# Two graph layers on one core: the second layer's first gathers read a copy of its table that lacks three node tiles

## The chip, the core and the metric

The kernel runs on one core of a Trainium2 chip. The metric is device microseconds of one execution, the median of the timed runs. The engines are named as in the profile: PE (TensorE, the matrix products), DVE (VectorE), ACT (ScalarE), POOL (GpSimd) and SP (SyncE, which here only issues transfers). Every engine works through its own queue in order and waits at semaphores for the others.

## What is computed

The inputs are 6250 nodes with 128 features and 200,000 edges, sorted by their destination. Two layers follow each other, both over the same edges:

```python
h = relu(layernorm(x))
z = (h @ W).reshape(N, 8, 16)                 # layer 0: graph attention, 8 heads
e = leaky_relu(el[src] + er[dst], 0.2)
a = exp(e - segment_max(e, dst)[dst])
agg = segment_sum(z[src] * a, dst) / segment_sum(a, dst)
x = x + agg + bias
h = relu(layernorm(x))
s, v = h @ W_up (scalar and vector part)      # layer 1: messages by tensor product
w0..w3 = silu(silu(edge_feats @ A1 + b1) @ A2 + b2) @ A3
m = products of s[src], v[src], edge_attrs and w0..w3   # 256 numbers an edge
x = x + segment_sum(m, dst) / 10 @ W_out
```

What matters here is `z[src]` and `s[src], v[src]`: for every edge a row of a table is fetched by the number of its source node. The sources are in no order, so layer 1 can read any row of its table from its first edge on.

## The kernel before

**Tables and gathers.** `t0` (136 floats a node) and `t1` (128 floats a node) are tables in DRAM. `t0` is complete before layer 0 starts. `t1` is written by layer 0, node tile by node tile. The edges form 1563 tiles of 128; 16 tiles are a block, and there are 98 blocks. `gather` (L830) issues one indirect DMA on POOL for each edge tile: 128 rows of the table into one tile's place of a buffer. Buffers come from `z_pool`, five of them, each for one block; block 0 of layer 0 has a buffer of its own, `z_first`. `gathered` takes the next buffer of the pool and fills it. In 31 blocks (`by_row`, every third) the last tile isn't gathered; SP fetches its 128 rows one by one (`rows_by_row`, L1067), three blocks ahead.

**Layer 0.** The loop over `g` (L1346) handles one group of tiles, nearly always a block, in each pass: `logits` of group g, the maxima over each destination, `weights`, `weighted` and `sums` of group g - 1, and every second pass the node work for the node tile that group g - 2 completed: `node_x`, `node_d`, `node_h`, `node_t` and `node_s`, which ends with `sv`, a node tile's 128 rows of `t1`. `node_out` (L1281) stores `sv` into `t1`, from SP, at the top of the next pass. There are 50 node tiles. After the loop the last four groups are written out by hand (L1410 to L1464). Tile 46 is stored first there, tile 47 after the sums of group 95 have been carried on, and tiles 48 and 49 together at the very end. Block 97 is cut into a group of 3 tiles and one of 8.

**Layer 1.** It works in units of four edge tiles (391 of them). For each unit: `network`, one step of the edge network for the next block (`p_h` in PSUM); `tensor_weights`, the last product of that network; `messages` (DVE, L1532 to L1541), which reads the gathered rows; `one_hot`; and `sums1` (PE, L1549), which adds the unit's messages to its block's sums. `edge_rows` loads the edge inputs of a block from SP. `take_rows(b + 2)` stands at the first unit of block b. `node1` and `node_out1` close a node tile.

**Order.** The queues of PE, DVE, ACT and SP keep the order of the program within a layer (`manual_schedule`). POOL's gathers keep theirs too, and run ahead as far as buffers are free. Tiles of DRAM are tracked like others: a gather from `t1` waits for every store to `t1`.

**Pools.** What both layers or layer 0 alone need stands in the pool `fconst`, which stays open to the end. `s_pool` and `row_pool` are opened after a pool named `fbuild`, in which the masks are built, has been closed; they lie where it lay.

Of the kernel before, what the change touches and what calls it, by code (L numbers as in the profile page):

```python
# [18 lines left out]
P = 128  # L19
H = 8  # L20
D = 16
F = H * D
# [3 lines left out]
MW = 8 * MU  # L26
# [3 lines left out]
KB = 16  # L30
# [705 lines left out]
W0 = 32  # L736
PRE = 1.0 / math.sqrt(MU)
# [4 lines left out]
def tile_even_edges(  # L742
# [28 lines left out]
    nc = tc.nc  # L771
    NX = xp.shape[0] // P
    TU = n_tiles
    TG = -(-TU // P)
# [5 lines left out]
    keep = ctx.enter_context(tc.tile_pool(name="keep", bufs=1))  # L780
    t0 = dram.tile([NX * P - W0, ZW], F32, name="ft0")
    t1 = dram.tile([NX * P - W0, P], F32, name="ft1")

    def rows(i):

# [41 lines left out]
        nc.vector.scalar_tensor_tensor(mr[:m], mv[:m, :, 0:1], -1.0, rs[:m], op0=OP.mult, op1=OP.mult)  # L827
        return rs, mr

    def gather(to, table, tiles, width):  # L830
        for k, t in enumerate(tiles):
            nc.gpsimd.indirect_dma_start(  # L832
                out=to[:, k, :width], out_offset=None, in_=table,
                in_offset=bass.IndirectOffsetOnAxis(ap=src_col[:, t : t + 1], axis=0))
        return to
# [128 lines left out]
def even_edges(tc, v):  # L964
    nc = tc.nc
    NX, TU, TG, NB, KT, MC = (v[k] for k in (
        "NX", "TU", "TG", "NB", "KT", "MC"))
    t0, t1, ident, eps, er3, z_first, dstt, nums = (v[k] for k in (
        "t0", "t1", "ident", "eps", "er3", "z_first", "dstt", "nums"))
    xp, dstc, y4, f8, bias, out, moments, deviation, normal, gather, tiles_of = (v[k] for k in (  # L970
        "xp", "dstc", "y4", "f8", "bias", "out", "moments", "deviation", "normal", "gather", "tiles_of"))
    with ExitStack() as ctx:
        const = ctx.enter_context(tc.tile_pool(name="fconst", bufs=1))
        z_pool = ctx.enter_context(tc.tile_pool(name="fz", bufs=5))

        def gathered(table, tiles, width):
            return gather(z_pool.tile([P, KB, ZW], F32, name="g"), table, tiles, width)

        iota = const.tile([P, P], F32, name="fiota")
        nc.sync.dma_start(iota, nums[:, NB * KB + TG : NB * KB + TG + P])  # L980
        jp = const.tile([P, P], F32, name="fjp2")
        nc.sync.dma_start(jp, nums[:, NB * KB + TG + P :])
        rsel = const.tile([P, P // KB, P], BF, name="frsel")
        nc.sync.dma_start(rsel, v["rsel"])
        x_all = const.tile([P, NX, P], F32, name="fx_all")
        bias_b = const.tile([P, F], F32, name="fbias_b")
# [16 lines left out]
        identb = const.tile([P, P], BF, name="fidentb")  # L1003
        nc.vector.tensor_copy(identb, ident)

        er3o = const.tile([P, NX, 3, H], BF, name="fer3o")
        nc.sync.dma_start(er3o[:WB, :, :, :], er3[WB:, :, :, :])
        nc.sync.dma_start(er3o[WB:, : NX - 1, :, :], er3[:WB, 1:, :, :])
        shift = const.tile([P, 3, P], F32, name="fshift")
        for k, by in enumerate((-H, P - H, H)):  # L1010
            nc.vector.tensor_single_scalar(shift[:, k, :], jp, float(by), op=OP.is_equal)
        masks = const.tile([P, TG, MC], BF, name="fmasks")
# [25 lines left out]
        s_pool = ctx.enter_context(tc.tile_pool(name="fs", bufs=16))  # L1038

        by_row = [b for b in range(3, NB - 2) if b % 3 == 0]
        row_pool = ctx.enter_context(tc.tile_pool(name="frow", bufs=3))
        at = [const.tile([P, P], I32, name=f"fat{i}") for i in range(2)]
        with tc.tile_pool(name="fat_ps", bufs=1, space=PSUM) as at_ps:
            col = const.tile([P, P], F32, name="fcol")
# [44 lines left out]
        def finish(b, p_u, width, carry, agg, pool):  # L1091

            if b % 2 == 0:
                agg = pool.tile([P, MW], F32, name="agg")
            o = agg[b % 2 * WB : b % 2 * WB + WB, :width]
            if carry is None:
                nc.vector.tensor_copy(o, p_u[:WB, :width])
            else:
                nc.vector.tensor_add(o, p_u[:WB, :width], carry[:, :width])
            carry = pool.tile([WB, MW], F32, name="carry")  # L1100
            nc.scalar.copy(carry[:, :width], p_u[WB:, :width])
            return carry, agg


        in_order = {mybir.EngineType.PE, mybir.EngineType.DVE, mybir.EngineType.Activation,
                    mybir.EngineType.SP}
        with tc.manual_schedule(engines=in_order), \
# [160 lines left out]
            def node_s(u):  # L1268
                i, n, p_n = u["i"], u["n"], u["p_n"]
                for j in range(n):  # L1270
                    nc.tensor.matmul(p_n[:, 2 + j, :], u["h_t"][:, j, :], wup, start=True, stop=True)
                sv = u["sv"] = l0n.tile([P, 2, P], F32, name="sv")
                nc.scalar.activation(sv[:, :n], p_n[:, 2 : 2 + n], AF.Copy, scale=PRE)

            def node_out(u):
                i, n, sv = u["i"], u["n"], u["sv"]
                first = i * P - W0
                if i == 0:
                    nc.sync.dma_start(t1[: P - W0, :], sv[W0:, 0, :])
                else:  # L1280
                    nc.sync.dma_start(t1[first : first + n * P].rearrange("(j p) f -> p j f", p=P),  # L1281
                                      sv[:, :n])

            groups = [(b, 0, KB) for b in range(NB - 1)]
            cut = min(3, KT[-1] - 1)
# [1 line left out]
            shift_to = {}  # L1287
            for _, _, kt in groups:
                if kt * H not in shift_to:
                    sh = const.tile([P, P], F32, name=f"fshift{kt}")  # L1290
# [45 lines left out]
            er_sum(cs[0])  # L1336
            for q in range(4):
                ends_of(cs[1], q)
            st = {"ends": const.tile([P, 2, MW], F32, name="fends")}
# [71 lines left out]
            for n in late:  # L1411
                node_out(n)
            with_bias(NX - 2, 2)

            logits(c3)
            masks_of(c2)
# [45 lines left out]
            node_out(u)  # L1462
            for step in (node_d, node_h, node_t, node_s, node_out):
                step(w)  # L1464


        with tc.manual_schedule(engines=in_order), \
# [106 lines left out]
            both = l1n.tile([P, 2, MW], F32, name="both", bufs=1)  # L1574
            nc.vector.memset(both[WB:, 1, :], 0.0)

            blk = [{} for _ in range(NB)]
            us = [{"b": b, "k0": k0, "m": min(4, KT[b] - k0)}
                  for b in range(NB) for k0 in range(0, KT[b], 4)]
            NU = len(us)  # L1580

            def take_rows(b):
                if b < NB:
                    blk[b]["z"] = gathered(t1, range(b * KB, b * KB + KT[b] - (b in by_row)), P)

            rows, rows_until.n, late = rows_by_row(1, t1, P), 0, []
            for b in range(2):
                edge_rows(b)
                take_rows(b)
            for step in range(4):  # L1590
                network(0, step)
            tensor_weights(us[0])
# [4 lines left out]
            for i, u in enumerate(us):  # L1597
                b, k0, m = u["b"], u["k0"], u["m"]
                if k0 == 0:
                    take_rows(b + 2)  # L1600
                    filled(1, b, blk[b]["z"], P)
                    edge_rows(b + 2)
                if k0 == 4:
                    while late:
                        node_out1(late.pop())
                rows_until(rows, b + (k0 + 4) / KB)
                if b + 1 < NB:
                    network(b + 1, k0 // 4)
# [177 lines left out]
```

## Time and profile before

| | |
|---|---|
| timed runs, median of 3 | 3916.27 us (3915.74 to 3917.14) |
| profiled execution | 6201.12 us, span 6199.2 us |
| mean granted PE clock, profiled | 0.692 |
| PE busy, share of the span | 2970.3 us, 48% |
| POOL busy | 2919.2 us, 47% |
| DVE busy | 2207.9 us, 36% |
| ACT busy | 1390.7 us, 22% |

The profiled execution is 1.58 times as long as a timed run. Its durations of single instructions can be used; its waits have to be read with care, because a timed run has 2285 us less of them. In the timeline each line gives the start in us from the beginning of the span, the length, the engine, the line of the kernel, the operation and its tiles; the brackets give the idle time before it and what ended that. In the trace both tables are called `ft` (`ft0`, `ft1`), the table of source numbers `fsrc`, and gathered buffers `g` or `fz_first`. [...]

### The profile page before, as it was taken

The numbers are of one execution on the slowest core, as the hardware profiler recorded it, in microseconds if no ns is written. First come the engines' busy times: TensorE is split into PE (matmuls) and PEld (weight loads), VectorE is DVE, ScalarE is ACT, GpSimd is POOL, SyncE is SP. The second block draws the span as 40 slices with busy tenths as digits, with TensorE's granted clock in tenths as the row PEclk, the third lists the DMA queues.
The fourth block names the chain that finished last, engine by engine and source line by source line (L and its number), as shares of the span: only waits on it lengthen the run. The fifth ranks groups of instructions, "written<-read, shape, count | busy, mean of one in ns | idle before, by whom it ended". The sixth has DMA issues, their size and how long they took to land. (4 is left out here: it accounts for less than half of the span.)

```text
span 6199.2 us, 62249 instructions
## 1 busy us (share of the span) xinstructions
PE 2970.3 (48%) x14593; PEld 2462.3 (40%) x14593; DVE 2207.9 (36%) x5379; ACT 1390.7 (22%) x3612; POOL 2919.2 (47%) x3096
## 2 busy tenths in 40 slices
PE   2444434334443434444445555555555555555557
PEld 1333333333333333433334444444444444444445
DVE  3332323223232322232234334443344434443346
ACT  2212112112121212122112222222222222222223
POOL 6354454544445444454534444444444444444442
PEclk6666666656666665665677777777777777777778
DMA  5111111111111111111111111111111111111110
GB/s 133 31 41 39 39 41 40 40 41 39 39 40 42 40 39 40 39 41 39 39 30 35 38 38 37 37 37 37 38 37 36 35 39 38 36 36 37 39 38 25
DMA packets 188124, 249.35 MB, mean 40 GB/s; under 512 B 77888, under 2 KB 137952, under 8 KB 187744
## 3 DMA queue, kind: packets, MB, share of 16 engines
q0 software_dynamic: 98048, 207.27, 14.1%
q1 hardware_dynamic: 89408, 37.92, 2.4%
q8 instruction: 118, 1.93, 0.1%
q14 instruction: 262, 2.15, 0.1%
q10 hardware_dynamic: 288, 0.07, 0.0%
HBM read 234.73 MB, written 9.99 MB: 39 GB/s over the span
## 5 line engine op out<-in xcount | busy, mean ns | idle before, releaser
L832 POOL DMA_INDIRECT g<-ft,fsrc x3048 | 2885.4, 947 | 3174.9 <-issue 1510.7
L1549 PE MATMUL p_u<-mj,s 128*128 128x256 f32 x3126 | 925.2, 448 | 719.5 <-DVE mj L1541 601.3
L1549 PEld LDWEIGHTS p_u<-mj,s 128*128 128x128 f32 x3126 | 679.9, 225 | 905.1 <-DVE mj L1541 656.2
L1221 PE MATMUL p_u<-g,s 128*128 128x136 f32 x3062 | 621.5, 382 | 42.5 <-issue 39.6
L1221 PEld LDWEIGHTS p_u<-g,s 128*128 128x128 f32 x3062 | 588.6, 285 | 48.9 <-issue 44.9
L1534 DVE TENSOR_TENSOR p_w<-g,p_w 128x128 f32<-128x128 f32 x391 | 114.7, 293 | 1278.6 <-ACT p_w L1516 1099.6
L1516 ACT ACTIVATE p_w<-p_w,yb 128x64 f32<-128x64 f32 x1563 | 451.1, 289 | 475.1 <-remote 250.9
L1149 PEld LDWEIGHTS <-d 128*128 128x128 bf16 x1563 | 99.2, 113 | 845.1 <-ACT d L1140 512.0
L1512 PE MATMUL p_w<-fa3p,h 128*128 128x256 f32 x1564 | 427.4, 398 | 0.0
L1140 ACT CAST d<-p_d 128x512 bf16<-128x512 f32 x391 | 228.1, 587 | 881.3 <-remote 746.2
L1502 ACT ACTIVATE h<-p_h,fb 128x512 f32<-128x512 f32 x196 | 134.9, 688 | 1167.9 <-remote 841.8
L1512 PEld LDWEIGHTS p_w<-fa3p,h 128*128 128x128 f32 x1564 | 306.3, 206 | 142.3 <-issue 103.1
L1560 PE MATMUL p_n<-fwout,m_t 128*128 128x128 f32 x192 | 57.1, 451 | 561.6 <-ACT m_t L1558 561.6
L1138 PE MATMUL p_d<-fident,s 128*128 128x128 f32 x1563 | 320.1, 357 | 5.2 <-issue 5.2
L1216 DVE TENSOR_TENSOR g<-g,pe 128x1024 f32<-128x1024 f32 x193 | 226.2, 1213 | 226.2 <-ACT g L1207 155.4
L1499 PE MATMUL p_h<-h,fa2p 128*128 128x512 f32 x392 | 245.9, 714 | 125.2 <-ACT h L1497 98.7
L1532 DVE TENSOR_TENSOR vy<-g,p_i 128x384 f32<-128x384 f32 x391 | 215.0, 550 | 218.0 <-ACT p_i L1491 216.3
L1497 ACT ACTIVATE h<-p_h,fb 128x512 f32<-128x512 f32 x196 | 134.6, 687 | 698.2 <-PE p_h L1495 391.4
L1155 DVE TENSOR_REDUCE p_n<-p_er 128x128 f32<-128x384 f32 (+1 forms) x97 | 54.7, 563 | 663.6 <-remote 257.3
L1149 PE MATMUL p_er<-fer,d 128*128 128x24 bf16 x784 | 55.3, 185 | 467.7 <-ACT d L1140 285.2
L1086 DVE TENSOR_TENSOR s<-p_i,fdloc 128x512 f32<-128x512 f32 x391 | 269.0, 688 | 14.0 <-ACT h L1497 14.0
L1138 PEld LDWEIGHTS p_d<-fident,s 128*128 128x128 f32 x1563 | 258.2, 192 | 39.3 <-issue 30.6
(185 smaller groups left out, 3478.5 us busy)
## 6 DMA issues: line engine op xcount, KB each, us to landing
r<-ft SPq DMA_DIRECT2D x3968, 0.5 KB
r<-ft SPq DMA_DIRECT2D x3968, 0.5 KB
g<-ft,fsrc POOLq DMA_INDIRECT x3048
ft<-in_e_f_dram SPq DMA_DIRECT2D x98, 64.0 KB
yb<-in_e_y_dram SPq DMA_DIRECT2D x98, 32.0 KB
fx_all<-in_e_xp_dram SPq DMA_DIRECT2D x48, 64.0 KB
ft<-sv SPq DMA_DIRECT2D x47, 64.0 KB
out_dram<-fx_all SPq DMA_DIRECT2D x47, 64.0 KB
```

Of the source, the lines that this page charges most:

```text
L832: nc.gpsimd.indirect_dma_start(out=to[:, k, :width], out_offset=None, in_=table, in_offset=bass.IndirectOffsetOnAxis(ap=src_col[:, t : t + ...
L1086: nc.vector.tensor_tensor(s[:, :m], iota[:, None, :].to_broadcast([P, m, P]), dloc[:, t : t + m].unsqueeze(2).to_broadcast([P, m, P]), OP. ...
L1138: nc.tensor.transpose(p_d[:, k, :], c["s"][q][:, k, :], ident)
L1140: nc.scalar.copy(d[:, :m], p_d[:, :m])
L1149: nc.tensor.matmul(c["p_er"][:, 4 * q + k].rearrange("p s h -> p (s h)"), c["d", q][:, k, :], er_w, start=True, stop=True)
L1216: nc.vector.tensor_mul(zh, zh, p_a[:, k0 : k0 + m].unsqueeze(3).to_broadcast([P, m, H, D]))
L1221: nc.tensor.matmul(c["p_u"][:, :ZW], c["s"][k // 4][:, k % 4, :], c["z"][:, k, :], start=c["o"] + k == 0, stop=c["o"] + k == KT[c["b"]] - 1)
L1499: nc.tensor.matmul(p_h.rearrange("p q e -> p (q e)"), a2p, c["h1"].rearrange("p q e -> p (q e)"), start=True, stop=True)
L1512: nc.tensor.matmul(w[:, k : k + n].rearrange("p k a u -> p (k a u)"), c["h2"][q // 4][:, q % 4, :], a3p[:, :n].rearrange("p k f -> p (k f) ...
L1516: nc.scalar.activation(w[:, k, ::2, :], w[:, k, ::2, :], AF.Copy, scale=c["yb"][:, k0 + k, 0:1])
L1532: nc.vector.tensor_mul(vy, v_n, y_p)
L1549: nc.tensor.matmul(blk[b]["p_u"][:, :MW], u["s"][:, k, :], u["mj"][:, k, :], start=k0 + k == 0, stop=k0 + k == KT[b] - 1)
```

## The change

A second table, `t1z`, is written beside `t1`. Node tiles 0 to 46 are stored into both. Tiles 47, 48 and 49 of `t1z` are zero: zeros are stored there once, in the setup. The rows of these three tiles stay in SBUF (`sv_late`).

The first 24 edge tiles of layer 1 are gathered from `t1z` in place of `t1`: block 0 into `z_first`, and half of block 1 into a buffer of the pool. These gathers stand in the program after tile 46's stores. An edge whose source lies in the last three node tiles gets a row of zeros this way, and the missing row is added on the chip: for four edge tiles at a time, PE spreads the source numbers over the partitions (4 products), DVE compares them with the numbers of the three tiles' nodes (3 comparisons), PE multiplies the resulting zeros and ones by `sv_late` (12 products), and DVE adds the result to the gathered rows. This runs one to two units ahead of the unit that reads the rows, six times in all. The other tiles of block 1 and all later ones come from `t1`.

The pools are ordered anew: `s_pool` and `row_pool` are opened before `fbuild`, and what layer 0 alone needs (`rsel`, `masks`, `er3o` and others) moves from `fconst` to a pool `l0c`, closed before layer 1.

The diff, cut to what the prediction speaks of:

```diff
+    t1z = dram.tile([NX * P - W0, P], F32, name="ft1z")
...
-    def gather(to, table, tiles, width):
-        for k, t in enumerate(tiles):
+    def gather(to, table, tiles, width, first=0):
+        for k, t in enumerate(tiles, first):
...
         z_pool = ctx.enter_context(tc.tile_pool(name="fz", bufs=5))
+        s_pool = ctx.enter_context(tc.tile_pool(name="fs", bufs=16))
+        row_pool = ctx.enter_context(tc.tile_pool(name="frow", bufs=3))
+        of_l0 = ctx.enter_context(ExitStack())
+        l0c = of_l0.enter_context(tc.tile_pool(name="l0c", bufs=1))
...
+        NL, NE = 3, 24
+        LATE = NX - NL
...
-        rsel = const.tile([P, P // KB, P], BF, name="frsel")
+        rsel = l0c.tile([P, P // KB, P], BF, name="frsel")
...
+            zeros = build.tile([P, NL, P], F32, name="fzeros")
+            nc.vector.memset(zeros, 0.0)
+            nc.sync.dma_start(t1z[LATE * P - W0 :].rearrange("(j p) f -> p j f", p=P), zeros)
...
+        sv_late = const.tile([P, NL, P], F32, name="fsv_late")
...
-                sv = u["sv"] = l0n.tile([P, 2, P], F32, name="sv")
-                nc.scalar.activation(sv[:, :n], p_n[:, 2 : 2 + n], AF.Copy, scale=PRE)
+                if i < LATE:
+                    sv = u["sv"] = l0n.tile([P, 2, P], F32, name="sv")[:, :n]
+                else:
+                    sv = u["sv"] = sv_late[:, i - LATE : i - LATE + n]
+                nc.scalar.activation(sv, p_n[:, 2 : 2 + n], AF.Copy, scale=PRE)
...
-                if i == 0:
-                    nc.sync.dma_start(t1[: P - W0, :], sv[W0:, 0, :])
-                else:
-                    nc.sync.dma_start(t1[first : first + n * P].rearrange("(j p) f -> p j f", p=P),
-                                      sv[:, :n])
+                for table in (t1, t1z) if i < LATE else (t1,):
+                    if i == 0:
+                        nc.sync.dma_start(table[: P - W0, :], sv[W0:, 0, :])
+                    else:
+                        nc.sync.dma_start(
+                            table[first : first + n * P].rearrange("(j p) f -> p j f", p=P), sv)
...
             with_bias(NX - 2, 2)
+            early = {0: gather(z_first, t1z, range(KB), P),
+                     1: gathered(t1z, range(KB, NE), P)}
...
+        of_l0.close()
...
+            place = l1n.tile([P, NL], F32, name="place", bufs=1)
+            for j in range(NL):
+                nc.vector.tensor_scalar(place[:, j : j + 1], jp[:, 0:1], -1.0,
+                                        float((LATE + j) * P - W0), op0=OP.mult, op1=OP.add)
+            src_f = l1n.tile([P, NE], F32, name="src_f", bufs=1)
+            nc.vector.tensor_copy(src_f, v["src_col"][:, :NE])
+
+            def late_ends(t):
+
+                if t < NE:
+                    p_h = l1_ps.tile([P, 4, P], F32, name="p_h")
+                    for k in range(4):
+                        nc.tensor.matmul(p_h[:, k, :], src_f[:, t + k : t + k + 1].to_broadcast([P, P]),
+                                         ident, start=True, stop=True)
+                    oh = late_ends.of[t] = l1n.tile([P, NL, 4, P], F32, name="oh")
+                    for j in range(NL):
+                        nc.vector.tensor_scalar(oh[:, j], p_h, place[:, j : j + 1], None,
+                                                op0=OP.is_equal)
+
+            late_ends.of = {}
+
+            def late_rows(t):
+                if t < NE:
+                    z, k0, oh = blk[t // KB]["z"], t % KB, late_ends.of.pop(t)
+                    p_n = l1_ps.tile([P, 4, P], F32, name="p_n", bufs=1)
+                    for k in range(4):
+                        for j in range(NL):
+                            nc.tensor.matmul(p_n[:, k, :], oh[:, j, k, :], sv_late[:, j, :],
+                                             start=j == 0, stop=j == NL - 1)
+                    z = z[:, k0 : k0 + 4, :P]
+                    nc.vector.tensor_add(z, z, p_n)
...
             def take_rows(b):
-                if b < NB:
+                if b in early:
+                    blk[b]["z"] = gather(early[b], t1, range(max(b * KB, NE), b * KB + KB), P,
+                                         max(NE - b * KB, 0))
+                elif b < NB:
                     blk[b]["z"] = gathered(t1, range(b * KB, b * KB + KT[b] - (b in by_row)), P)
...
                 take_rows(b)
+            for t in (0, 4):
+                late_ends(t)
+            late_rows(0)
             for step in range(4):
                 network(0, step)
...
                     tensor_weights(us[i + 1])
+                late_ends(4 * (i + 2))
                 messages(u)
+                late_rows(4 * (i + 1))
```

More of the change, by code (lines that the diff above doesn't have):

```diff
@@ L967, in even_edges @@
         "NX", "TU", "TG", "NB", "KT", "MC"))
-    t0, t1, ident, eps, er3, z_first, dstt, nums = (v[k] for k in (
-        "t0", "t1", "ident", "eps", "er3", "z_first", "dstt", "nums"))
+    t0, t1, t1z, ident, eps, er3, z_first, dstt, nums = (v[k] for k in (
+        "t0", "t1", "t1z", "ident", "eps", "er3", "z_first", "dstt", "nums"))
     xp, dstc, y4, f8, bias, out, moments, deviation, normal, gather, tiles_of = (v[k] for k in (
@@ L974, in even_edges @@
         z_pool = ctx.enter_context(tc.tile_pool(name="fz", bufs=5))
+        s_pool = ctx.enter_context(tc.tile_pool(name="fs", bufs=16))
+        row_pool = ctx.enter_context(tc.tile_pool(name="frow", bufs=3))
+        of_l0 = ctx.enter_context(ExitStack())
+        l0c = of_l0.enter_context(tc.tile_pool(name="l0c", bufs=1))
         def gathered(table, tiles, width):
             return gather(z_pool.tile([P, KB, ZW], F32, name="g"), table, tiles, width)
+        NL, NE = 3, 24
+        LATE = NX - NL
+        sv_of = {}
         iota = const.tile([P, P], F32, name="fiota")
@@ L982, in even_edges @@
         nc.sync.dma_start(jp, nums[:, NB * KB + TG + P :])
-        rsel = const.tile([P, P // KB, P], BF, name="frsel")
+        rsel = l0c.tile([P, P // KB, P], BF, name="frsel")
         nc.sync.dma_start(rsel, v["rsel"])
         x_all = const.tile([P, NX, P], F32, name="fx_all")
-        bias_b = const.tile([P, F], F32, name="fbias_b")
+        bias_b = l0c.tile([P, F], F32, name="fbias_b")
         nc.sync.dma_start(bias_b, bias.to_broadcast([P, F]))
@@ L1002, in even_edges @@
         dloc = const.tile([P, NB * KB], F32, name="fdloc")
-        identb = const.tile([P, P], BF, name="fidentb")
+        identb = l0c.tile([P, P], BF, name="fidentb")
         nc.vector.tensor_copy(identb, ident)
-        er3o = const.tile([P, NX, 3, H], BF, name="fer3o")
+        er3o = l0c.tile([P, NX, 3, H], BF, name="fer3o")
         nc.sync.dma_start(er3o[:WB, :, :, :], er3[WB:, :, :, :])
         nc.sync.dma_start(er3o[WB:, : NX - 1, :, :], er3[:WB, 1:, :, :])
-        shift = const.tile([P, 3, P], F32, name="fshift")
+        shift = l0c.tile([P, 3, P], F32, name="fshift")
         for k, by in enumerate((-H, P - H, H)):
             nc.vector.tensor_single_scalar(shift[:, k, :], jp, float(by), op=OP.is_equal)
-        masks = const.tile([P, TG, MC], BF, name="fmasks")
+        masks = l0c.tile([P, TG, MC], BF, name="fmasks")
         with tc.tile_pool(name="fbuild", bufs=1) as build:
@@ L1036, in even_edges @@
                 nc.scalar.activation(masks[:, g, :], eq[:, g, :], AF.Copy, bias=-BIG, scale=BIG)
-        s_pool = ctx.enter_context(tc.tile_pool(name="fs", bufs=16))
+            zeros = build.tile([P, NL, P], F32, name="fzeros")
+            nc.vector.memset(zeros, 0.0)
+            nc.sync.dma_start(t1z[LATE * P - W0 :].rearrange("(j p) f -> p j f", p=P), zeros)
         by_row = [b for b in range(3, NB - 2) if b % 3 == 0]
-        row_pool = ctx.enter_context(tc.tile_pool(name="frow", bufs=3))
         at = [const.tile([P, P], I32, name=f"fat{i}") for i in range(2)]
         with tc.tile_pool(name="fat_ps", bufs=1, space=PSUM) as at_ps:
-            col = const.tile([P, P], F32, name="fcol")
+            col = l0c.tile([P, P], F32, name="fcol")
             n = NB - 1
@@ L1289, in even_edges @@
                 if kt * H not in shift_to:
-                    sh = const.tile([P, P], F32, name=f"fshift{kt}")
+                    sh = l0c.tile([P, P], F32, name=f"fshift{kt}")
                     nc.vector.tensor_single_scalar(sh, jp, float(H - kt * H), op=OP.is_equal)
@@ L1338, in even_edges @@
                 ends_of(cs[1], q)
-            st = {"ends": const.tile([P, 2, MW], F32, name="fends")}
+            st = {"ends": l0c.tile([P, 2, MW], F32, name="fends")}
             nc.vector.memset(st["ends"], 0.0)
```

## The prediction

> **What bounds the kernel now.** I read the page's groups first, then the waits, then the timeline of GpSimd at the border of the layers, then that of the other engines there. The page (a group: busy time, mean ns of one, idle time before) and the waits (total, times, longest):
>
> ```profile
> span 6199.2 us, 62249 instructions
> L832 POOL DMA_INDIRECT g<-ft,fsrc x3048 | 2885.4, 947 | 3174.9 <-issue 1510.7
> ```
>
> ```profile
> POOL g L832 <- DVE mj L1541: 824.1, 63, 40.3
> ACT h L1502 <- remote: 841.8, 84, 26.8
> ```
>
> The profiled execution took 6201.12 us, the timed runs 3916.27 (median), 1.58 times less, so the trace can't be scaled; it has to be asked which of its limits also holds in a timed run. GpSimd's gathers do. The timeline round the border (start, length, engine; idle before and its releaser in brackets):
>
> ```profile
> 2959.96 0.94 POOL L832 DMA_INDIRECT g<-ft,fsrc  x1 [0.30 <-issue]
> 3006.51 0.95 POOL L832 DMA_INDIRECT g<-ft,fsrc  x1 [45.61 <-DMA ft<-sv]
> 3007.76 0.95 POOL L832 DMA_INDIRECT g<-ft,fsrc  x1 [0.30 <-issue]
> ...
> 3059.04 0.95 POOL L832 DMA_INDIRECT g<-ft,fsrc  x1 [0.30 <-issue]
> ```
>
> Between 3006.51 and 3059.04 lie 42 gathers: 1.2507 us each, wherever nothing holds GpSimd up. 3064 gathers (3048 and 16 into fz_first, the first at 42.4 us) take 42.4 + 3063 x 1.2507 = 3873.3 us to the start of the last. To this come the hole at the border and what follows the last gather. The end: 0.95 us of the gather, 2.3 us of landing (below), and the chain of the last three tiles, which runs from 6187.11 to 6199.2 in the trace, 12.1 us: 15.3. The hole, worked out below for a GpSimd that never waits for buffers: 28.0. Sum 3916.6, with the 1.9 us between span and profiled time 3918.5, and 3916.27 was measured (0.06%). I conclude that a timed run is GpSimd's queue from end to end, and that the trace's additional 2285 us are waits that a timed run doesn't have (ACT's idle time put down to "remote" is the largest that no engine explains; it comes where gathers run without a gap).
>
> The hole is one wait: the first gather of layer 1 reads t1, so it waits until the last sv store has landed. Lines that carry it:
>
> ```profile
> 2946.72 0.28 DVE L1163 TENSOR_TENSOR e_s<-g,p_n 128x128 f32<-128x128 f32 x1
> 2964.05 0.34 SPq L1281 DMA_DIRECT2D ft<-sv  x1
> 2969.57 0.29 DVE L1163 TENSOR_TENSOR e_s<-g,er 128x128 f32<-128x128 f32 x1
> 2981.83 0.23 DVE L1163 TENSOR_TENSOR e_s<-g,er 128x64 f32<-128x64 f32 x1
> 2999.48 4.71 SPq L1281 DMA_DIRECT2D ft<-sv  x2
> ```
>
> They are the logits of block 95, the store of node tile 46, the logits of block 96 and of the last group, the stores of tiles 47 and 48 to 49 (the second ends at 3004.19; GpSimd starts 2.3 us later: my landing time).
>
> Let s be the start of layer 0's last gather. With GpSimd always busy, block 95's last gather starts 27 before it and has landed at s - 33.8 + 0.95 + 2.3 = s - 30.5. From there by the distances in the trace: tile 46's store is issued at +17.3 (s - 13.2), block 96's logits come at +22.9 (s - 7.7; it landed at s - 10.5), the last group's 12.3 later (s + 4.6; landed at s + 3.3), the first gather of layer 1 36.9 after block 96's logits: s + 29.2. Without the hole it would be s + 1.25. So the hole is 28.0 in a timed run, against 45.3 in the trace.
>
> **The change part by part.**
>
> 1. Early gathers (-28.0). 16 tiles go into fz_first, 8 into a new g, from t1z. The built program has them right behind layer 0's last gather, waiting for t1z's stores up to node tile 46 and no later one. The copy's store follows tile 46's own by 0.4 us, so it has landed at s - 13.2 + 0.4 + 0.4 + 2.3 = s - 10: no wait. fz_first has been free since block 0. The g tile is the one that group 94 used, whose sums end at about the same time as tile 46's store: free before its turn at s + 21. So 24 gathers, 24 x 1.2507 = 30.0 us, fill the hole; tile 24, from t1, starts at max(s + 31.3, s + 29.2). Before it started at s + 29.2 + 30.0 = s + 59.2. Gain 27.9, say 28.0. It can't pass 30.0, the price of the 24.
>
> A rule of the Trainium skill speaks against this: "GPSIMD Engine Reference", Key points, says that GpSimd shares its SBUF interfaces with VectorE and contends with its two-port modes and its operations on two SBUF inputs. The tail of layer 0 is full of DVE work. By the rule the 24 would be slower than 1.25 each by an amount it doesn't give. The rows: gathers start 1.25 apart from 2951.20 to 2959.96, where DVE was busy 11.5 of 20 us (2940 to 2960), and 1.25 apart from 3060 to 3080, where it did nothing. I take the rows: nothing added.
>
> 2. Late rows on TensorE and VectorE, six groups of four tiles (cover: GpSimd's lead). Each group: 4 products 128x128, 3 comparisons 128x512, 12 products 128x128, 1 addition 128x512. TensorE's nearest row is L1495, 4 such products:
>
> ```profile
> 3007.69 2.05 PE L1495 MATMUL p_h<-ft,fa1p 128*128 128x128 f32 x8 [4.32 <-DMA ft<-in_e_f_dram]
> 3123.92 1.05 PE L1495 MATMUL p_h<-ft,fa1p 128*128 128x128 f32 x8
> ```
>
> and the windows (busy time by engine, then granted clock, DMA share, GB/s):
>
> ```profile
> 3060.00:3080.00 20.00, 0.00 (x0) 0.00 (x0) 0.00 (x0) 0.69 (x1) 15.13 (x16) 0.52 0.21 53
> 3120.00:3140.00 20.00, 12.95 (x59) 9.94 (x57) 9.65 (x25) 4.75 (x12) 13.55 (x15) 0.84 0.17 43
> ```
>
> 16 products are 4.2 us at clock 0.84 and 8.2 at about 0.5. Which? The trace's layer 1 starts cold, with long pauses. The skill's "TensorE: Matmul & The Clock Gate", Part 1, gives full clock after about 3.4 us of work without pause; here the added work itself keeps TensorE busy. By the row beside it (cold) the six groups cost 49 us, by the rule 25. I take 25, and keep 49 for the range. VectorE: 3 x 0.69 (L1086, the same size read from PSUM) + 0.69 = 2.8 us a group.
>
> What hides it: without pauses a unit of layer 1 takes 4.1 us (DVE's L1541, 6124.61 to 6165.64, is 10 units), GpSimd's four tiles 4 x 1.2507 x 0.98 = 4.9 (SP brings 31 of 1563 tiles). Layer 1's compute starts at s + 26. Unit 0 now has a group ahead of its network: about 8 us later than the 18.9 of before, s + 53. Five more units at 4.1 + 4.2: s + 95, and block 1's last two: s + 103. GpSimd first needs a freed buffer at block 6 (five g tiles), tile 95, at s + 1.25 + 95 x 1.2507 = s + 120. So 17 us remain; at the cold price (24 us more) block 1 ends at s + 127 and GpSimd waits 7. Unit 6 starts at s + 95, its tiles have landed at s + 38: the lag of 57 us is won back at 0.8 us a unit: 72 of 385 units. Cost 0; without that cover, 29 (rival A).
>
> 3. 47 more stores of 64 KB on SP in layer 0, 0.42 each with their gap: 20 us of SP's time in all. SP carries 128 row transfers per three blocks; its best stretch in the trace is 12 in 3.96 us (0.33 each, 14 us a block), a usual one 77 in 48.05 (0.62, 27 a block). GpSimd gives 19.55 a block, so the sum above needs rows at 0.45 or less; rows run three blocks ahead. I take 0; the other end is 20. In layer 1 the rows start as before while tiles come 28 us sooner: they suffice up to about 0.42.
>
> 4. Waits. VectorE's addition now waits for TensorE, with messages and the next one_hot behind it; that is inside the unit prices. The two products of p_h and p_n take turns with network and node1 in the same banks. The new order puts one edge_rows load before the last t1 store on SP; it waits for the same last TensorE product, 0.4 us, which is as long as ACT needs for sv: 0 to 0.4, below the 2.1 us that tile 24 has to spare. fzeros (128x384 memset, store) and the moved pools fall before 80 us, where GpSimd needs no freed buffer until tile 95, at 161: 0, at most a us either way.
>
> Sum: -28.0. Timed: 3916.3 - 28.0 = 3888.3.
>
> **The rivals.**
>
> A, slower: layer 1 is paced by compute, not by gathers, in timed runs too. For: in the trace GpSimd waited 824.1 us for L1541. Against: the sum of 3918.5, and units of 4.1 us. Place: the six first units. Price 8 + 5 x 4.2 = 29, since unit 0 before didn't wait for its rows: about 3945 (cold 3969). It decides from a pace of 4.9 us a unit; between 4.77 and 4.9 the lag is won back in part and the gain is only partly lost.
>
> B: the gathers stretch the tail beside which they now run. Stretched by X, the gain is 30.0 - X once X passes 2.1. For: ACT's pauses of 10 to 27 us under gap-free gathers in the trace. Against: timed runs gather without a gap all through layer 0 and keep pace. With one pause of 10 to 18: 3896 to 3904.
>
> C: SP paces layer 0, the 20 us count: 3908.
>
> D: the early gathers wait for the last tiles after all: 3916. The built order speaks against it.
>
> **How the numbers follow.** Main case 0.76 (3885 to 3893); B 0.09; C 0.04; D 0.03; A 0.08. The range 3883 to 3904 holds the main case and most of B. A measurement here tells 0.2% (7.8 us) from no change: faster 0.84, same 0.07, slower 0.09.
>
> **What would show it.** Right: GpSimd goes from ft0 to ft1z at 0.30 us of idle time; the hole before the first ft1 gather is under 3 us, or as long as the tail is stretched. The traced span itself says little, since its layers are held up by pauses: the tail may well be stretched there (B). Wrong if: the wait on L1281's store stands before the first ft1z gather; GpSimd waits for block 1's L1541 at block 6; the timed runs lie above 3908.

## The result and the profile after

The changed kernel takes 3888.89 us (median of 4 timed runs, 3887.98 to 3890.92), the kernel before took 3916.64 us in the runs beside it (4 runs, 3915.74 to 3917.14): a ratio of 0.9931, 95% interval 0.9919 to 0.9944, or 27.75 us less. The prediction had been 28.0 us less than 3916.3.

On one of the chips used here every kernel that was run, the one before included, takes about 6300 us with long idle times of ACT, as in the profile shown before the change, so times from there are compared only with each other; everything else, the profile after included, comes from executions of 3880 to 4040 us, in which a profiled execution is as long as a timed one (3888.67 us, span 3886.9).

The page of the kernel after, its first line and the group of the gathers (busy time, mean ns of one, idle time before them):

```profile
span 3886.9 us, 62701 instructions
L833 POOL DMA_INDIRECT g<-ft,fsrc x3024 | 2856.7, 945 | 922.4 <-issue 858.3
```

and its waits (engine, line, what it waited for: total, times, longest):

```profile
POOL g L833 <- issue: 860.1, 2820, 0.3
DVE e_s L1176 <- DMA g<-ft,fsrc: 568.2, 91, 9.2
DVE vy L1553 <- DMA g<-ft,fsrc: 258.0, 163, 3.5
```

From gather to gather GpSimd never stands still for more than 0.3 us, the step from one to the next. (The 824.1 us that GpSimd waited for DVE in the profile before belong to that slow execution, and their absence is not the change's doing: the trace of `plumbing` below, whose gathers are those of before, hasn't got them either.) Others wait for GpSimd: the first instruction of `logits` in layer 0, and the first of `messages` in layer 1. So GpSimd is the bound in both layers.

The timeline of GpSimd at the border (start, length, line, operation; idle time before it and what ended that), first and last gather of each table:

```profile
1958.13 0.95 POOL L833 DMA_INDIRECT g<-ft,fsrc  x1 [0.30 <-issue]
1959.38 0.94 POOL L833 DMA_INDIRECT fz_first<-ft1z,fsrc  x1 [0.30 <-issue]
...
1988.10 0.94 POOL L833 DMA_INDIRECT g<-ft1z,fsrc  x1 [0.30 <-issue]
1989.35 0.94 POOL L833 DMA_INDIRECT g<-ft,fsrc  x1 [0.30 <-issue]
```

The first line is layer 0's last gather, the prediction's s, here 1958.13. The next 24 read `ft1z`, the last line is tile 24 from `ft1`. No idle time is longer than 0.31 us: the hole of before (45.61 us in the profile shown there) has gone completely. The work that the hole had waited for goes on beside the gathers. Lines picked from the timelines of DVE and SP, the logits of blocks 95, 96 and of the last group, and the stores of tile 46 and of tiles 48 and 49:

```profile
1926.96 0.29 DVE L1176 TENSOR_TENSOR e_s<-g,p_n 128x128 f32<-128x128 f32 x1 [7.56 <-DMA g<-ft,fsrc]
...
1941.65 0.34 SPq L1298 DMA_DIRECT2D ft<-sv  x1
1942.03 1.38 SPq L1298 DMA_DIRECT2D ft1z<-sv  x1
...
1947.28 0.28 DVE L1176 TENSOR_TENSOR e_s<-g,er 128x128 f32<-128x128 f32 x1
...
1961.33 0.23 DVE L1176 TENSOR_TENSOR e_s<-g,er 128x64 f32<-128x64 f32 x1 [2.02 <-DMA g<-ft,fsrc]
...
1983.38 0.43 SPq L1298 DMA_DIRECT2D ft<-fsv_late  x1
```

The rows of a gather land some time after its instruction ends: the last group's logits wait for the last gather of layer 0 and start 2.25 us after its end (1958.13 + 0.95, then 1961.33).

### The profile page after: what moved, and what is told of

The parts are those of the page before. It is cut to its first block, busy times and chain, and to the rows that moved or that the text cites. A ratio compares the mean times of both kernels' runs of the same rounds, so it can differ in the third digit from the quotient of the medians.

```text
span 3886.9 us, 62701 instructions
## 1 busy us (share of the span) xinstructions
PE 2848.8 (73%) x14785; PEld 2401.2 (62%) x14785; DVE 2224.5 (57%) x5408; ACT 1396.8 (36%) x3612; POOL 2913.0 (75%) x3096
## 5 line engine op out<-in xcount | busy, mean ns | idle before, releaser
L833 POOL DMA_INDIRECT g<-ft,fsrc x3024 | 2856.7, 945 | 922.4 <-issue 858.3
L1570 PE MATMUL p_u<-mj,s 128*128 128x256 f32 x3126 | 789.9, 397 | 217.9 <-DVE mj L1562 216.5
L1570 PEld LDWEIGHTS p_u<-mj,s 128*128 128x128 f32 x3126 | 588.9, 196 | 385.7 <-DVE mj L1562 310.9
L1151 PE MATMUL p_d<-fident,s 128*128 128x128 f32 x1563 | 384.7, 411 | 0.0
L1151 PEld LDWEIGHTS p_d<-fident,s 128*128 128x128 f32 x1563 | 312.4, 225 | 37.6 <-issue 26.3
L1144 ACT COPY mk<-p_m 128x385 f32<-128x385 f32 (+1 forms) x99 | 47.6, 481 | 781.3 <-PE p_m L1141 781.2
L1179 PE MATMUL pe<-fident,e_s 128*128 128x128 f32 x98 | 39.1, 399 | 326.2 <-DVE e_s L1177 326.2
L1097 DVE TENSOR_TENSOR s<-p_n,fdloc 128x512 f32<-128x512 f32 x391 | 266.1, 682 | 6.7 <-ACT sv L1289 3.4
L1516 PE MATMUL p_h<-ft,fa1p 128*128 128x128 f32 x1568 | 217.2, 283 | 63.3 <-DMA ft<-in_e_f_dram 63.1
L1516 PEld LDWEIGHTS p_h<-ft,fa1p 128*128 128x128 f32 x1568 | 210.6, 198 | 83.9 <-issue 65.3
```

The lines of the kernel that those rows point to most:

```text
L833: nc.gpsimd.indirect_dma_start(out=to[:, k, :width], out_offset=None, in_=table, in_offset=bass.IndirectOffsetOnAxis(ap=src_col[:, t : t + ...
L1097: nc.vector.tensor_tensor(s[:, :m], iota[:, None, :].to_broadcast([P, m, P]), dloc[:, t : t + m].unsqueeze(2).to_broadcast([P, m, P]), OP. ...
L1151: nc.tensor.transpose(p_d[:, k, :], c["s"][q][:, k, :], ident)
L1516: nc.tensor.matmul(p_h[:, q, :], a1p[:, q0 + q, :], c["ft"], start=True, stop=True)
L1570: nc.tensor.matmul(blk[b]["p_u"][:, :MW], u["s"][:, k, :], u["mj"][:, k, :], start=k0 + k == 0, stop=k0 + k == KT[b] - 1)
```

## The experiments

### The change without the early gathers (plumbing)

All that the change adds around the early gathers is kept: the second table and its 47 stores, the zeros, the new places of the pools.

```diff
-            early = {0: gather(z_first, t1z, range(KB), P),
-                     1: gathered(t1z, range(KB, NE), P)}
+            early = {}
...
-                if t < NE:      # late_ends and late_rows
+                if t < 0:
```

> Everything that the change adds around the early gathers, without them: t1z and its 47 stores, the zero rows, the moved pools; all gathers of layer 1 from t1, no late rows. Theory: costs nothing, 3916.6 (within 2). Rival (SP paces layer 0, or the new places of the pools make a wait): up to 20 more, 3936.

Measured: 3916.24 us against 3917.58, ratio 0.9998 (0.9990 to 1.0007). The surroundings cost nothing. Since this kernel's gathers are those of before, its trace also shows the hole of before in an execution of ordinary length, first GpSimd's gathers, then the last group's logits and the last store:

```profile
1956.88 0.94 POOL L833 DMA_INDIRECT g<-ft,fsrc  x1 [0.30 <-issue]
1986.46 0.94 POOL L833 DMA_INDIRECT g<-ft,fsrc  x1 [28.63 <-PE p_h L1515]
1987.71 0.94 POOL L833 DMA_INDIRECT g<-ft,fsrc  x1 [0.30 <-issue]
...
1959.98 0.23 DVE L1176 TENSOR_TENSOR e_s<-g,er 128x64 f32<-128x64 f32 x1 [1.99 <-DMA g<-ft,fsrc]
...
1983.75 0.43 SPq L1298 DMA_DIRECT2D ft<-fsv_late  x1
```

The second line is the first gather of layer 1. Of its 28.63 us of idle time 0.30 is the usual step, so the hole is 28.33 us, the only one in the kernel:

```profile
POOL g L833 <- issue: 862.1, 2827, 0.3
POOL g L833 <- PE p_h L1515: 28.6, 1, 28.6
```

The releaser that is named, a product of PE, is not the cause, since a gather doesn't read what that product writes: the last store to `ft1` starts at 1983.75 and takes 0.43 us, and the gather starts 2.28 us after its end, as it started 2.3 us after it in the profile shown before and 2.31 in early8b below. The reader sees here that the instruction named behind a wait can be one that merely ended at that time.

### Fewer and more early tiles (early8b, early32b)

```diff
-        NL, NE = 3, 24
+        NL, NE = 3, 8
...
-            early = {0: gather(z_first, t1z, range(KB), P),
-                     1: gathered(t1z, range(KB, NE), P)}
+            early = {0: gather(z_first, t1z, range(min(NE, KB)), P)}
```

> 8 tiles early, as in early8, again, because there the kernel before itself took 6294 us with long idle times of ACT, and GpSimd's queue wasn't what set the time. Theory: where before takes about 3917, 8 x 1.25 = 10.0 us are gained, so 3907; GpSimd's idle time before its first gather from t1 18 to 20 us. Rival (something else in the change brings the gain): about 3889.

Measured: 3906.78 us against 3916.48, ratio 0.9975 (0.9965 to 0.9985): 9.7 us less, where 8 x 1.25 gives 10.0. The trace shows the rest of the hole behind the eighth early gather; what is named as its end is again not a cause, a load that landed then:

```profile
1970.57 0.94 POOL L833 DMA_INDIRECT fz_first<-ft1z,fsrc  x1 [0.30 <-issue]
1989.08 0.94 POOL L833 DMA_INDIRECT fz_first<-ft,fsrc  x1 [17.57 <-DMA yb<-in_e_y_dram]
```

17.57 - 0.30 = 17.3 us, a little below the 18 to 20 expected. With 32 tiles (`NL, NE = 3, 32`, else as the change):

> 32 tiles early, as in early32, again for the same reason. Theory: the hole of 28 us is filled after 23 tiles, so 3888.5, as with 24; two more groups of late rows stay hidden (late2 hid 16 us more). Rival (1.25 a tile goes on): 3879.

Measured: 3888.53 us, ratio 0.9929 (0.9916 to 0.9943), the same as with 24 (3888.89). The last early gather and the first from `ft1`:

```profile
1998.39 0.94 POOL L833 DMA_INDIRECT g<-ft1z,fsrc  x1 [0.30 <-issue]
1999.64 0.94 POOL L833 DMA_INDIRECT g<-ft,fsrc  x1 [0.30 <-ACT p_w L1537]
```

`ft1` was readable about 11 us before 1999.64 (its last store starts at 1985.46, and 0.43 + 2.3 us later it has landed), so the last early tiles replaced gathers that could have been made from `ft1`. The gain is 1.25 us a tile as far as the hole reaches, and nothing beyond. A cause that doesn't count tiles, such as the moved pools or a few early rows for the first units, would have given 3889 or 3892 to 3900 with 8 tiles; it is excluded.

### The late rows' work left out, doubled, five times (no_late, late2, late5)

`no_late` has only the second edit of `plumbing`. The other two repeat the 12 products of `late_rows`, each repetition overwriting the sums of the one before:

```diff
-                    for k in range(4):
+                    for k in [*range(4)] * 2:      # late5: * 5
                         for j in range(NL):
                             nc.tensor.matmul(p_n[:, k, :], oh[:, j, k, :], sv_late[:, j, :],
```

> The change without the late rows' work on TensorE and VectorE (no products, comparisons and additions): the rows of the last three node tiles stay zero for the edges of the first 24 tiles. Theory: the work lies in GpSimd's lead, so 3888.9, as with it. Rival (part of its 45 to 50 us still shows): earlier by what shows, 3880 to 3887.

> Each group's 12 products of the late rows done twice, with the same result: about 2.7 us more in each of 6 groups by the trace after (24 halves in 2.84 at clock 0.91), 16 in all. Theory: block 1's messages end about 98 us after the start of layer 0's last gather in the trace after, GpSimd needs its buffer at 120, so 16 more still hide: 3888.9. Rival (no cover is left): 3905.

> Each group's 12 products five times: 48 more in each of 6 groups, about 2.7 x 4 x 6 = 65 us. Theory: block 1's messages end at 98 + 65 = 163 after the start of layer 0's last gather, GpSimd waits for its buffer from 120 on: 43 us later in the end, since GpSimd never waits again: about 3932 (3920 to 3940). Rival (the lag of compute decides from its first microsecond on): 3954. Rival (the lag never matters): 3889.

Measured: 3888.01 us without the work, 3887.95 doubled, 3918.79 five times (before: 3917.58; ratios 0.9927, 0.9929 and 1.0004). Without or with twice the work, the time is that of the change within its runs: the work is hidden. Five times is too much. GpSimd's gathers of late5 before and at block 6, with DVE's last message of block 1, which frees the buffer:

```profile
2077.58 0.94 POOL L833 DMA_INDIRECT g<-ft,fsrc  x1 [0.30 <-issue]
...
2108.70 0.55 DVE L1562 TENSOR_TENSOR mj<-g,p_w 128x384 f32<-128x384 f32 x1
...
2109.52 0.94 POOL L833 DMA_INDIRECT g<-ft,fsrc  x1 [31.00 <-DVE mj L1562]
```

GpSimd reaches block 6 at 2109.52 - 30.70 = 2078.8, 119.9 us after the start of layer 0's last gather (1958.9 in this trace); the prediction had put that at 120. It waits 30.7 us, once, and the kernel ends 3918.79 - 3888.89 = 29.9 us later. So the wait that rival A names is real: its place is block 6, its price is what compute is later than s + 120. (A's reason, that layer 1 is paced by compute throughout, is not: after this one wait GpSimd isn't held up again.) The change stays 22 us short of it. The last message of block 1 in the trace after (s = 1958.13, so it ends at s + 97.9), and in that of no_late (s = 1957.11, s + 66.7):

```profile
2055.45 0.55 DVE L1562 TENSOR_TENSOR mj<-g,p_w 128x384 f32<-128x384 f32 x1
```

```profile
2023.25 0.54 DVE L1562 TENSOR_TENSOR mj<-g,p_w 128x384 f32<-128x384 f32 x1
```

The late rows thus cost compute 31.2 us up to there, and all of it lies in GpSimd's lead.

My expectation for late5 was too high by 13 us, and late2's block 1 ended 3.6 us later than that of the change, not 16. The reason is in PE's pauses and its clock. The trace after, one unit of layer 1 in steps of 1 us (window; length, PE busy and its instructions, granted clock, DMA share, GB/s):

```profile
2013.00:2014.00 1.00, 0.80 (x8) 1.00 0.25 66
2014.00:2015.00 1.00, 0.00 (x0) 1.00 0.23 61
2015.00:2016.00 1.00, 0.23 (x1) 1.00 0.10 14
2016.00:2017.00 1.00, 1.00 (x5) 0.73 0.45 59
2017.00:2018.00 1.00, 1.00 (x4) 0.50 0.29 67
2018.00:2019.00 1.00, 1.00 (x5) 0.50 0.28 67
2019.00:2020.00 1.00, 1.00 (x7) 0.56 0.22 54
2020.00:2021.00 1.00, 1.00 (x7) 1.00 0.14 35
```

PE stands still for about 2 us, because its next products need the messages and DVE makes these only after the comparisons, which had waited for PE. Then, from about 0.7 us after PE has gone on, the clock is at half for about 3.4 us, while PE is fully busy. The products of `sums1` in this unit and in the next one of the trace after, then those of the second unit in late2:

```profile
2015.77 3.14 PE L1570 MATMUL p_u<-mj,s 128*128 128x256 f32 x8 [1.96 <-DVE mj L1562]
...
2026.71 1.99 PE L1570 MATMUL p_u<-mj,s 128*128 128x256 f32 x8 [1.96 <-DVE mj L1562]
```

```profile
2018.80 1.89 PE L1570 MATMUL p_u<-mj,s 128*128 128x256 f32 x8
```

PE has four such pauses before `sums1`, 1.96 us each (they end at 2004.83, 2015.77, 2026.71 and 2035.96). After three of them the clock falls to 0.50, after the third, the second line above, it stays at 1.00. So the length of the pause alone doesn't decide; what else does isn't shown by these runs. In late2 PE never stands still there, the clock stays at 1.00, and the second unit takes 9.7 us from message to message (2007.94 to 2017.64) where it takes 10.9 in the kernel with half the work (2004.23 to 2015.16). The first added products went into time that PE had lost anyway: by an estimate from these figures, four pauses of 1.96 us and three stretches of 3.4 us at half clock are 7.8 + 3 x 1.7 = 12.9 us, and late2's block 1 ended 12.4 us before what was expected. In late5 the clock is at 1.00 from 2000 to 2112 us, too. "TensorE: Matmul & The Clock Gate", Part 1, in the Trainium skill, gives about 3.4 us of work until the clock is full again, which fits the stretch at half clock in the windows; it also ties the fall to a whole idle window of that length, while here about 2 us of standing still preceded it, and not each time.

### A version that might beat both (rows38, rows38_l1)

If the gathers are the time, tiles that SP fetches row by row save 1.25 us each. These kernels give SP 35 tiles a layer and not 31, `rows38` in both layers, `rows38_l1` in layer 1 alone (through a list for each layer).

```diff
-        by_row = [b for b in range(3, NB - 2) if b % 3 == 0]
+        by_row = [-(-8 * k // 3) for k in range(1, NB) if -(-8 * k // 3) < NB - 2]
...
-            while rows_until.n < (block + 3) * P / 12 and next(rows, 0) is None:
+            while rows_until.n < (block + 3) * 12 and next(rows, 0) is None:
```

> A tile by rows on SP in 3 of 8 blocks, not 1 of 3, in both layers (35 and not 31 tiles a layer leave GpSimd's queue; SP's pace 12 groups of rows a block). Theory (GpSimd's queue is the time): 8 x 1.25 = 10 us less, 3879, if SP can carry 48 rows a block. Rival (SP is nearly full in layer 0: there it sends 85 rows in 39.8 us for two blocks, 0.41 each, so 96 rows and three stores would need about 40.7 where GpSimd needs 39.0): SP paces layer 0 and it comes out slower, 3890 to 3960.

> The same in layer 1 alone, where SP sends its rows at 0.34 to 0.38 us with idle time between. Theory: 4 x 1.25 = 5 us less, about 3883.9. Rival (SP or ACT's copies hold layer 1 up): 3889 or more.

Measured: 4031.07 and 4009.42 us, against 3916.48: slower by 2.9 and 2.4%. Both theories missed badly. The rivals had the direction right, but that of rows38 missed too: it put the loss into layer 0 and at 3960 at most, while layer 1 alone costs 120.5 us against the change (4009.42 to 3888.89) and layer 0 only 21.65 more. The line of SP that loads the rows' offsets into registers, from the trace after (duration in ns, lowest, median and highest):

```profile
L1074 SPq TENSOR_LOAD <-fat x248: 1894/2172/2378, 68.9 to 3697.2; - x124
```

I had counted 0.34 to 0.38 us for a row and left out these loads, 2.17 us for every 32 rows. With them, at 3 tiles in 8 blocks a block of layer 1 costs SP 48 x 0.33 + 1.5 x 2.17 + 2.5 other transfers of 0.47 = 20.3 us, where GpSimd takes 19.5; at 1 in 3 it is 42.7 x 0.33 + 1.33 x 2.17 + 1.2 = 18.2. SP's timeline in rows38_l1 shows one such block, from one load of edge inputs to the next:

```profile
3005.11 0.37 SPq L1498 DMA_DIRECT2D ft<-in_e_f_dram  x1
3005.58 0.37 SPq L1500 DMA_DIRECT2D yb<-in_e_y_dram  x1
3008.23 3.88 SPq L1079 DMA_DIRECT2D r<-ft  x12
3012.21 0.37 SPq L1591 DMA_DIRECT2D out_dram<-fx_all  x1
3012.68 14.31 SPq L1079 DMA_DIRECT2D r<-ft  x36
3027.09 0.37 SPq L1498 DMA_DIRECT2D ft<-in_e_f_dram  x1
```

22.0 us for this block; over all 98 the kernel is 4005.8 - 3886.9 = 118.9 us longer, 1.2 a block. In this block SP has no time left over (the gap before 3008.23 holds a load of offsets); for the other blocks the sum above is an estimate. The edge inputs stand behind the rows in SP's queue, so the network's first product comes late. Its waits in layer 1 (from 2100 us on), first the trace after, then rows38_l1:

```profile
PE p_h L1516 <- DMA ft<-in_e_f_dram: 61.2, 25, 5.1
```

```profile
PE p_h L1517 <- DMA ft<-in_e_f_dram: 290.1, 87, 5.0
```

ACT's copies, which the rival named beside SP, are unlikely to be the cause: ACT itself waits 711.5 us for these products there, 530.2 in the trace after. In layer 0 (rows38 against rows38_l1: 21.65 us) a full SP shows in another place: ACT's `sv` waits 327.3 us, 38 times, for the store to `ft1z` that still holds its buffer. The change itself stays the fastest version that was run.

### The chip on which ACT stands still (before_again, early8, early16, early32)

The kernel before, and the change with 8, 16 and 32 early tiles, as above (16 tiles were run on this chip only).

> The kernel before, unchanged, with another profile, because its first profiled execution took 1.58 times a timed run. Theory (a timed run is GpSimd's queue end to end, one hole at the border of 28.0 us, no pauses): a profiled execution of about 3917 us, GpSimd's idle time before its gathers 0.3 us each but for one hole of 27 to 29 us that ends with the last store of t1, 1.25 us from gather to gather. Rival (the pauses belong to this kernel and the change took them away): again over 4000 us, with ACT's waits put down to remote and GpSimd waiting for DVE in layer 1.

> Only 8 tiles come early from t1z (two groups of late rows). Theory: the gain is the number of early gathers times 1.25 us as long as that is below the hole of 28: 8 x 1.25 = 10.0, so 3906.6. Rival 1 (the gain comes from something else that the change brings, such as a shorter border on SP or the moved pools): as the full change, about 3889. Rival 2 (the rows of the first units, not GpSimd's time, are what counts, so a few early tiles bring most of it): 3892 to 3900.

> 16 tiles early (four groups of late rows). Theory: 16 x 1.25 = 20.0, so 3896.6. Rival 1: about 3889, as with 24. Rival 2: below 3896, less than 10 us gained over 8 tiles.

> 32 tiles early (eight groups of late rows). Theory: the hole is used up at 23 tiles (28.0/1.25), so 8 more bring nothing: 3888.9, and the two further groups of late rows lie in GpSimd's lead over compute (block 1 then done about 8 us later, still before GpSimd needs its buffer). Rival (the gain goes on growing by 1.25 a tile, because it isn't a hole that is filled): 3879. Rival (compute's lag decides): 3893 or more.

Measured: 6289.78 us (one run), 6298.77, 6292.31 and 6318.71, the kernel before in its own runs beside them 6293.81; ratios 1.0006 (0.9996 to 1.0015), 0.9999 (0.9988 to 1.0010) and 1.0045 (1.0032 to 1.0059). None of the theories' numbers could come out, since GpSimd's queue isn't the time on this chip. GpSimd's long waits after layer 0's last gather, in before_again to block 7, then in early32 to block 6:

```profile
3063.38 0.95 POOL L832 DMA_INDIRECT g<-ft,fsrc  x1 [48.27 <-DMA ft<-sv]
...
3179.27 0.95 POOL L832 DMA_INDIRECT g<-ft,fsrc  x1 [17.38 <-DVE mj L1541]
...
3209.17 0.95 POOL L832 DMA_INDIRECT g<-ft,fsrc  x1 [10.21 <-DVE mj L1541]
...
3268.93 0.95 POOL L832 DMA_INDIRECT g<-ft,fsrc  x1 [41.29 <-DVE mj L1541]
```

```profile
3035.50 0.94 POOL L833 DMA_INDIRECT fz_first<-ft1z,fsrc  x1 [6.34 <-issue]
...
3103.12 0.94 POOL L833 DMA_INDIRECT g<-ft,fsrc  x1 [27.97 <-PE p_h L1611]
...
3261.41 0.94 POOL L833 DMA_INDIRECT g<-ft,fsrc  x1 [79.96 <-DVE mj L1562]
```

The hole of 48.27 us shrinks to 6.34 and 27.97. But the waits for buffers, which are at blocks 5, 6 and 7 in before_again (there block 0 takes one of the five buffers, so block 5 is the first that needs one back), 68.9 us in all, become 79.96 at block 6 and 16.44 at block 7, 96.4 us: where compute sets the pace, what the gathers gain at the border is waited for at the next buffers, and more. The times fit that, but no run here takes ACT's idle times away on this chip, so what makes it 1.6 times slower, and whether anything else is behind the 0.45%, stays open. The kernel before took 6293.81 us here (40 runs) and 3917.58 and 3916.48 us (25 and 13 runs) on the two chips of the other experiments, so the long waits don't come from the kernel; they belong to this chip, or to its state at that time.

## Why the prediction was right

**A timed run is GpSimd's queue end to end: right.** From the trace of plumbing: the first gather starts at 41.26, the last at 3898.74, and (3898.74 - 41.26 - 28.33)/3063 is 1.2501 us from gather to gather (predicted 1.2507). The end from the last gather on is 3913.8 - 3898.74 = 15.1 us, in the trace after 3886.9 - 3870.95 = 15.95 (predicted 15.3).

**The hole: 28.33 us, predicted 28.0.** It was worked out from distances in a profile whose own hole was 45.3. In the trace after block 95's logits come at s - 31.2 (predicted s - 30.5), tile 46's store at s - 16.5 (s - 13.2), block 96's logits at s - 10.9 (s - 7.7), the last group's at s + 3.2 (s + 4.6), and `ft1` is readable at 1983.81 + 2.3, s + 28.0 (s + 29.2). Single distances are off by up to 3.3 us, because in the slower profile block 95's to 96's stretch was itself longer (22.9 us there, 20.3 here). It did no harm: the last group can't start before its gather has landed, and that counts from s. That the hole itself was met within 0.3 us is in part luck, for two errors cancel: in the trace of plumbing (s = 1956.88) the last group's logits come at s + 3.1, 1.5 us sooner than in the sum, which had taken the distance of the slow profile and not the landing at s + 3.3, and from there to the first gather of layer 1 it takes 26.5 us, 1.8 longer than the 24.7 of the slow profile.

**Early gathers: right.** Tile 24 starts at s + 31.2, predicted s + 31.3. No early gather waits for tile 46's copy. The rule of "GPSIMD Engine Reference" in the Trainium skill, Key points, on interfaces shared with VectorE, had no visible effect: 24 gathers beside the tail take (1989.35 - 1959.38)/24 = 1.249 us each, while DVE is busy 16.5 of these 30 us, and 1.250 is the mean of the whole kernel with DVE busy 57% of it. The row was the right choice.

**Late rows: hidden as predicted, prices a little off.** Three comparisons take 2.07 us and an addition 0.68, as predicted (0.69 each), 16 products 1.05 + 2.84 = 3.9 us at full clock (predicted 4.2). Unit 0 is done at s + 46.6 (predicted s + 53), unit 5 at s + 90.1 (s + 95), block 1 at s + 97.9 (s + 103). From unit 0 to unit 5 a unit takes 8.7 us (predicted 8.3). In no_late unit 0 is done at s + 40.4 and a unit takes 3.7 us up to unit 5, so a group costs unit 0 6.3 us (predicted 8) and each of the next five 5.0 (predicted 4.2), in all the 31.2 us above, where the sum had 29: it had no term for PE standing still until DVE is done, nor for the half clock after it. The rule of the skill's page (25 us for PE's part of six groups) was the better guide than the cold row (49). But PE doesn't stay busy as I had argued: the four pauses of 1.96 us came with the added work; no_late has one of 1.73 us in these units (1995 to 2024 us) and otherwise none above 0.62, and its clock is at 1.00 all through. That the cover came out at 22 us and not 17 comes mostly from unit 0, which without a group is done 4.5 us sooner than the slow profile had given (s + 26 + 18.9).

**The lag: won back more slowly than predicted.** I had 0.8 us a unit, 72 units, some 350 us. DVE waits for a gather before a message again only from 2600 us on (none before, 12 times from 2600 to 2900); 73 units from 2060.2 to 2398.3 take 4.63 us each, not 4.1, against 4.9 for their gathers. The term that was mis-sized is the unit's pace in pauseless work, taken from ten units at the end of the slow trace; why 4.63 and not 4.1 isn't shown. It costs nothing, as GpSimd is ahead, but the lead grows more slowly after block 6 than I had argued, and the pace is nearer to where A would decide (the prediction says 4.77; its own 57 us over 385 units, from 4.9, give 4.75).

**The rivals.** A is refuted for the change; late5 shows its wait to be real, and its point where it was put. B: from the last group's logits to the start of the last store 22.05 us pass beside the gathers (1961.33 to 1983.38), in plumbing, without gathers beside it, 23.8: nothing is stretched. C: 47 stores cost nothing (plumbing), but SP is nearer to its end than I had argued: in layer 0 of the trace after, 84 rows take 34.43 us, 0.41 each, the loads of offsets included, where I had named 0.45 as the point; rows38 asks for more rows than that leaves room for. D is excluded by the timeline.

## What to carry to other kernels

When one queue is the time from end to end, a hole in it is worth its full length and no more: count the items that fill it, and stop there. Price the work that pays for it against the lead of that queue, at the place where the queue first needs something back (here a buffer at block 6), because up to that place it is free and beyond it each microsecond counts. And before more work is moved to a helper queue such as SP's, sum up everything that it issues, register loads too: it may be over 90% full (here 18.2 of 19.5 us a block, by the sum above) without ever showing up as the bound.

## What I had not expected of the hardware

- PE's granted clock fell to 0.50 for about 3.4 us after PE had stood still for 1.96 us, in three of four such pauses, and doubling the products, which removed the pause, shortened that unit from 10.9 to 9.7 us.
- A load of 32 offsets into SP's registers takes 2.17 us, as long as 6.6 of the row transfers (0.33 us) that use them.
- The same program took 6294 us on one chip and 3916 to 3918 on others. Between the profiles before_again and plumbing a gather (947 against 945 ns) and ACT's `p_w` (288 in both) take as long, the products of `sums1` are longer (454 against 399 ns, at a mean granted clock of 0.689 against 0.802), and ACT stands still much longer.
